# Ten expert units' down products as seven products instead of eight, summed in PSUM, in a one-core perceiver layer

## The chip, the cores and the metric

The kernel is one program on one NeuronCore of a Trainium2 chip. The metric is the device time of that program in microseconds (us). Three runs of the kernel before gave 785.26, 785.72 and 786.43 us, median 785.72 us. The profile shows one further execution, instruction by instruction.

Engines are named as the profile names them: PE is TensorE's matrix multiplication and PEld its loading of the stationary operand, DVE is VectorE, ACT is ScalarE, POOL is GpSimd, SP the engine that issues most DMAs. SBUF is the on-chip memory, PSUM the accumulators that PE writes (eight banks of 512 fp32 columns).

## The reference, cut to what matters

T = 256 tokens of width D = 512 go through three residual blocks: a sigmoid cross-attention over 25,088 context rows, a causal self-attention with 16 heads of 64, and a mixture of experts. Everything is fp32. The change lies in the third:

```python
gu = x @ shared_gate_up_w                                  # shared: 1024 hidden
shared = _silu(gu[:, :Is]) * gu[:, Is:] @ shared_down_w
shared = shared * jax.nn.sigmoid(x @ shared_gate_w)
probs = jax.nn.softmax((x @ gate_w).astype(jnp.float32), axis=-1)
w, idx = jax.lax.top_k(probs, TOP_K)                       # 8 of 64 experts a token
w = w / jnp.sum(w, axis=-1, keepdims=True)
...
gu_e = jnp.einsum('ech,ehf->ecf', buf, expert_gate_up_w)
act = _silu(gu_e[..., :I]) * gu_e[..., I:]                 # I = 256 hidden
out_e = jnp.einsum('eci,eih->ech', act, expert_down_w)
y = out_e[e_flat, slot] * w_flat[:, None]                  # weight of the token
return (y + shared).reshape(B, S, H)
```

## The kernel before, in words

The first 551 us of the trace are the cross-attention, the next 60 the self-attention; neither is edited. In the self-attention a loop over e = 0..7 (two heads each) is pipelined by two steps: `scored(e)` puts scores into PSUM, DVE takes maxima, ACT exponentials, `divided(e, t)` lets POOL divide the exponentials `pe` by their sums (two POOL instructions a step), and `turned(e)` transposes them on PE one step later. `queries(e + 2)` in the same loop is the last reader of the turned input `anT`.

The mixture of experts works in *units* of 256 hidden columns. The shared expert is cut into four, s0 to s3. The routed experts are ranked by how many tokens chose them; the eight fullest, e0 to e7, are run for all 256 tokens, and a token that did not choose an expert has weight 0 for it. The seven next are run on gathered tokens (`seated`, `gathered`, and the `few_...` functions, with rounds of 32-slot quarters).

A unit has two parts. `gate_up` makes the hidden columns of all tokens, already transposed, [128 hidden, 2 halves, 256 tokens]: 16 products with a 128x128 stationary operand and 256 moving columns into two PSUM banks `ph`, then a sigmoid on ACT and two multiplications on DVE into `hT`. `down` multiplies them with the unit's down matrix `dn`: for each of the two token tiles, two products of 512 columns into a bank `pd`, and one DVE instruction (L1189) that multiplies with the tokens' weights (a column of `wsh` or `wso`) and adds to `y`. `run` pipelines this by one unit: `gate_up(n + 1)` comes before `down(n)`. Its `between` entries put other work behind unit i: `counted` (count and rank the experts, then load e0 to e2), `permuted` (the weights transposed to `wT`, and put into the order of rank, `wso`), the few experts' steps.

The order on each engine is the scheduler's: instructions in `in_turn` (tc.keep_in_program_order) keep the program's order, the others are placed one by one by its estimates. On the chip every engine then works strictly in that order. A tile pool gives a tag a fixed number of buffers; who takes a buffer waits for the last readers of its former content. `work` holds two buffers a tag (`tok`, `tokT`), `wpool` three for `gu` and `dn`, so that dn of unit n + 3 is loaded (by SP, in SP's order) once `down(n)` is done. In PSUM, `bank` deals four single banks in turn (`among_three` and `apart`), `banks` two pairs.

Of the kernel before, what the change touches and what calls it, by code (L numbers as in the profile page):

```python
# [9 lines left out]
F32 = mybir.dt.float32  # L10
# [11 lines left out]
def tile_perceiver_layer(  # L22
# [730 lines left out]
    def banks(name):  # L753
        return pairs.tile([P, 2, 512], F32, tag="two", name=name)
# [7 lines left out]
    def bank(name):  # L762
        turns[1] += 1
        return apart(name) if turns[1] % 4 == 0 else among_three(name)
# [20 lines left out]
    QUARTERS = dict(sorted(part for places in ROUNDS for part in places))  # L785
    FEW = len(QUARTERS)
    GROUP = 16
    weights = {}
    late = ctx.enter_context(tc.tile_pool(name="late", bufs=1))
    wpool = ctx.enter_context(tc.tile_pool(name="wpool", bufs=3))  # L790
    hidden = ctx.enter_context(tc.tile_pool(name="hidden", bufs=3))

# [11 lines left out]
        return gu, dn  # L804

    SP, ACT = (nc.sync, mybir.EngineType.SP), (nc.scalar, mybir.EngineType.Activation)

    def load_expert(k, gu=None, dn=None, by=SP):

        queue, engine = by  # L810
        if gu is None:
            gu = wpool.tile([P, ND, 2 * I], F32, tag="gu", name=f"gu_{k}")
        if dn is None:
            dn = wpool.tile([P, NI, D], F32, tag="dn", name=f"dn_{k}")
        e = nc.values_load(
            order[0:1, k : k + 1],
            engines=[engine],
            min_val=0,
            max_val=E - 1,
            skip_runtime_bounds_check_because="the number has been cut to six bits",  # L820
        )
        queue.dma_start(
            gu, e_gate_up[bass.ds(e, 1)].rearrange("o (c p) f -> p (o c) f", p=P)
        )
        queue.dma_start(dn, e_down[bass.ds(e, 1)].rearrange("o (c p) f -> p (o c) f", p=P))
        return gu, dn

    for k in range(NS):
# [248 lines left out]
    few = ctx.enter_context(tc.tile_pool(name="few", bufs=1))  # L1077


    wt = late.tile([P, NT, E], F32, tag="wt", name="wt")  # L1080
    wsh = late.tile([P, NT, 1], F32, tag="wsh", name="wsh")
    chosen_all = late.tile([P, NT, E], F32, tag="chosen", name="chosen_all")
    pls = []

# [19 lines left out]
    def choose(t):  # L1104
        lg = pls[t]
        top = small.tile([P, TOPK], F32, tag="top", name=f"top_{t}")
        nc.vector.max(top, lg[:, 0:E])
        rest = small.tile([P, E], F32, tag="rest", name=f"rest_{t}")
        nc.vector.match_replace(rest, top, lg[:, 0:E], LOWEST)
        chosen = chosen_all[:, t, :]  # L1110
        nc.vector.tensor_tensor(chosen, rest, lg[:, 0:E], ALU.not_equal)
        ntop = small.tile([P, 1], F32, tag="ntop", name=f"ntop_{t}")
        nc.vector.tensor_scalar(ntop, top[:, 0:1], -1.0, None, ALU.mult)
        ex = small.tile([P, E], F32, tag="ex", name=f"ex_{t}")
        in_turn(nc.scalar.activation(ex, lg[:, 0:E], AF.Exp, bias=ntop))
        nc.vector.tensor_mul(ex, ex, chosen)
        es = small.tile([P, 1], F32, tag="es", name=f"es_{t}")
        nc.vector.tensor_reduce(es, ex, AX.X, ALU.add)
        rs = small.tile([P, 1], F32, tag="res", name=f"res_{t}")
        nc.vector.reciprocal(rs, es)  # L1120
        nc.vector.tensor_scalar(wt[:, t, :], ex, rs, None, ALU.mult)
    def gate_up_products(n, halves, lo, hi, mark=lambda ins: ins):
        gu, _ = weights[n]
        for half, ph in enumerate(halves):
            for f in range(NI):
                col = half * I + f * P
                for c in range(ND):
# [10 lines left out]
    def gate_up(n, tiles_done=None):  # L1138
# [10 lines left out]
        nc.scalar.activation(hf, pg, AF.Sigmoid)  # L1149
        nc.vector.tensor_mul(hf, pg, hf)  # L1150
        nc.vector.tensor_mul(hf, pu, hf)
        return hT

# [16 lines left out]
    LAST_PARTS = WIDE_PARTS[:-1] + [(NT - 1, lo, lo + D // 2) for lo in range(0, D, D // 2)]  # L1172

    def down(n, hT, parts=WIDE_PARTS):
        _, dn = weights.pop(n)
        nm = f"{n[0]}{n[1]}"
        for t, lo, hi in parts:
            pd = banks(f"pd_{nm}_{t}_{lo}")[:, 0, 0 : hi - lo]
            for f in range(NI):
                nc.tensor.matmul(  # L1180
                    pd,
# [28 lines left out]
    def counted():  # L1210
# [33 lines left out]
            nc.vector.tensor_max(left[:, 0:1], left[:, 0:1], left[:, 1:2])  # L1244
        nc.vector.tensor_mul(left[:, 0:1], left[:, 0:1], nact)
        nc.vector.tensor_copy(active, left[:, 0:1])
        for k in range(3):
            weights["e", k] = load_expert(k)

    def permuted():  # L1250
# [4 lines left out]
        nc.tensor.matmul(pp[0:E, :E], lhsT=onesrow_sb, rhs=of, start=True, stop=True)  # L1255
        perm = late.tile([E, E], F32, tag="perm", name="perm")
        nc.vector.tensor_scalar(perm, pp[0:E, :E], number_sb, None, ALU.is_equal)
        pt = bank("pt_wt")
        for t in range(NT):
            nc.tensor.transpose(pt[0:E, t * P : (t + 1) * P], wt[:, t, :], ident)  # L1260
        wT = late.tile([E, T], F32, tag="wT", name="wT")
        nc.vector.tensor_copy(wT, pt[0:E, :T])
        pw = bank("pw_wt")
        for t in range(NT):
            nc.tensor.matmul(
                pw[:, t * E : (t + 1) * E],
                lhsT=wT[:, t * P : (t + 1) * P],
                rhs=perm,
                start=True,
                stop=True,  # L1270
            )
        nc.vector.tensor_copy(wso.rearrange("p t e -> p (t e)"), pw[:, : NT * E])

    run([("s", k) for k in range(NS)], {0: counted, 2: permuted})

# [160 lines left out]

    def few_spread():
        for t in range(NT):  # L1440
            pd = banks(f"pd_few_{t}")[:, 0, :]
            for r in range(NR):
                nc.tensor.matmul(
                    pd,
# [129 lines left out]
```

## Time and profile before

| what | value |
|---|---|
| median of three runs | 785.72 us (785.26 to 786.43) |
| profiled execution, own time | 786.12 us |
| its span, first to last instruction | 784.3 us |
| granted TensorE clock, mean | 0.999 |
| PE busy | 771.3 us (98%) |
| PEld busy | 612.4 us (78%) |
| DVE busy | 548.4 us (70%) |
| ACT busy | 202.4 us (26%) |
| POOL busy | 154.4 us (20%) |
| mixture of experts | from about 618 us of the span to its end |

The profiled execution took 0.40 us more than the median, and 1.82 us more than its span. A matmul of the kernel is fp32 and shows as two MATMUL and two LDWEIGHTS records, so the 16 products of a `gate_up` are a row of x32, and the four of a `down` a row of x8. A matmul's own duration overlaps the next one's; the distance from start to start is read from the chain or the timeline. "[0.30 <-DVE rsm L970]" behind a row is the idle time of that engine before it, and what ended it.

### The profile page before, as it was taken

The page shows a single profiled execution, that of the slowest core. Times are in us where ns is not written, and L with a number is a line of the kernel's source. Part 1 is how long each engine was busy: PE and PEld are TensorE (multiplying, and loading weights), DVE is VectorE, ACT ScalarE, POOL GpSimd, SP SyncE. Part 2 cuts the span into 40 slices and gives each one's busy share as a digit, 9 for nine tenths or more (in the row PEclk, how much of TensorE's full clock was granted, in tenths as well). Part 3 has the DMA queues.
Part 4 walks back from the last instruction along what each step waited for, and adds up shares of the span by engine and source line. Part 5 has one row for each costly group of instructions (what it writes and reads, how often), then busy time and mean ns, then how long its engine had stood idle before and what let it go on. Part 6 is the DMA issues. An engine that isn't in the chain of part 4 may idle for free.

```text
span 784.3 us, 12147 instructions
## 1 busy us (share of the span) xinstructions
PE 771.3 (98%) x4008; PEld 612.4 (78%) x4008; DVE 548.4 (70%) x1597; ACT 202.4 (26%) x485; POOL 154.4 (20%) x304
## 2 busy tenths in 40 slices
PE   8999999999999999999999999999999999999996
PEld 6888888888888888888888888889675676775563
DVE  5978878888788887887888878876655553513222
ACT  4222222222222222222222222222445310110110
POOL 3222223223222232232222322222123000000000
PEclk9999999999999999999999999999999999999999
DMA  9999999998786877878778788740600033399400
GB/s 246 268 233 257 260 226 293 240 213 195 206 196 169 211 186 191 206 171 212 188 177 211 178 198 201 171 115 1 221 22 2 1 134 132 113 369 392 148 1 30
DMA packets 153797, 140.86 MB, mean 180 GB/s; under 512 B 9088, under 2 KB 113280, under 8 KB 153728
## 3 DMA queue, kind: packets, MB, share of 16 engines
q1 hardware_dynamic: 152992, 139.49, 69.6%
q8 instruction: 34, 0.56, 0.3%
q10 hardware_dynamic: 672, 0.52, 0.2%
q14 instruction: 35, 0.29, 0.1%
q0 software_dynamic: 64, 0.00, 0.0%
HBM read 139.47 MB, written 0.52 MB: 178 GB/s over the span
## 4 chain that ended last, share of the span: by engine, by line
PE 96%; DVE 2%; ACT 1%; POOL 1%; issue 0%; ACTq 0%
PE xacc L572 36%; PE pk L355 22%; PE pz L373 11%; PE ph_e L1129 7%; PE pd_e L1180 4%; PE ph_s L1129 3%; PE pd_s L1180 2%; PE pa L844 2%; PE ph_few L1398 1%; PE pw L908 1%; PE py L727 1%; PE ps L934 1%; PE pi L211 1%; PE ptp L985 1%; PE po_few L1429 1%; PE pf L1375 1%
## 5 line engine op out<-in xcount | busy, mean ns | idle before, releaser
L572 PE MATMUL xacc<-T,S 128*128 128x172 f32 (+2 forms) x912 | 185.5, 308 | 0.0
L355 PE MATMUL pk<-cT,wkT_sb 128*128 128x384 f32 x512 | 175.5, 486 | 0.0
L572 PEld LDWEIGHTS xacc<-T,S 128*128 128x128 f32 x912 | 152.6, 190 | 20.3
L355 PEld LDWEIGHTS pk<-cT,wkT_sb 128*128 128x128 f32 x512 | 97.1, 190 | 54.4
L539 DVE TENSOR_TENSOR T<-ctx 128x172 f32<-128x172 f32 (+1 forms) x262 | 113.5, 434 | 0.0
L319 DVE STREAM_TRANSPOSE cT<-quarters 128x1536 f32<-128x1536 f32 x64 | 113.3, 1771 | 0.0
L539 POOL TENSOR_TENSOR T<-ctx 128x172 f32<-128x172 f32 x65 | 32.1, 493 | 385.5 <-PE xacc L572 379.3
L539 DVE TENSOR_TENSOR S<-zT 128x128 f32<-128x128 f32 x196 | 56.3, 287 | 72.7 <-ACT zT L382 72.7
L373 PE MATMUL pz<-qT,kT 128*128 128x256 f32 x392 | 106.0, 379 | 0.7 <-ACT kT L364 0.7
L382 ACT ACTIVATE zT<-pz 128x256 f32<-128x256 f32 (+1 forms) x131 | 64.2, 490 | 114.1 <-PE pz L373 114.1
L572 PE MATMUL xacc<-T,zT 128*128 128x173 f32 (+1 forms) x396 | 89.9, 308 | 0.0
L572 PE MATMUL xacc<-ctx,S 128*128 128x172 f32 x392 | 78.5, 309 | 0.0
L539 DVE TENSOR_TENSOR S<-zT,S 128x128 f32<-128x128 f32 x325 | 76.2, 285 | 0.0
L364 ACT ACTIVATE kT<-pk,bk 128x384 f32<-128x384 f32 (+1 forms) x66 | 38.2, 578 | 146.9 <-PE pk L355 146.9
L549 ACT COPY T<-ctx 128x170 f32<-128x170 f32 (+1 forms) x130 | 43.2, 334 | 125.4 <-PE xacc L572 125.4
L539 POOL TENSOR_TENSOR T<-ctx,T 128x170 f32<-128x170 f32 (+1 forms) x130 | 72.4, 576 | 2.2 <-PE xacc L572 2.2
L373 PEld LDWEIGHTS pz<-qT,kT 128*128 128x128 f32 x392 | 68.6, 190 | 4.8 <-ACT kT L364 1.3
L539 DVE TENSOR_TENSOR T<-ctx,T 128x172 f32<-128x172 f32 x195 | 65.4, 360 | 8.2 <-PE xacc L572 1.5
L572 PEld LDWEIGHTS xacc<-T,zT 128*128 128x128 f32 x396 | 66.4, 190 | 0.1
L572 PEld LDWEIGHTS xacc<-ctx,S 128*128 128x128 f32 x392 | 62.8, 190 | 0.0
L572 PE MATMUL xacc<-ctx,zT 128*128 128x170 f32 (+1 forms) x264 | 59.5, 307 | 0.0
L1129 PE MATMUL ph_e<-fT,gu 128*128 128x256 f32 x256 | 57.9, 381 | 0.0
(237 smaller groups left out, 716.2 us busy)
## 6 DMA issues: line engine op xcount, KB each, us to landing
ctx<-in_context SPq DMA_DIRECT2D x65, 768.0 KB, 5.3
quarters<-in_context SPq DMA_DIRECT2D x256, 192.0 KB, 6.3
gu<-in_e_gate_up SPq DMA_DIRECT2D x12, 1024.0 KB, 7.9
dn<-in_e_down SPq DMA_DIRECT2D x11, 512.0 KB, 6.1
gu_s<-in_s_gate_up SPq DMA_DIRECT2D x8, 512.0 KB, 5.9
a_wqT<-in_a_wqT SPq DMA_DIRECT2D x1, 2048.0 KB, 15.3
a_wout<-in_a_woutT SPq DMA_DIRECT2D x1, 2048.0 KB, 10.4
dn_s<-in_s_down SPq DMA_DIRECT2D x4, 512.0 KB, 7.7
```

The costliest lines, as they stand in the source:

```text
L211: nc.tensor.matmul(pi, lhsT=idle_sb[:, 0:P], rhs=idle_sb, start=True, stop=True)
L319: in_turn(nc.vector.transpose(new_turned(g), q.rearrange("p b (c r) -> p c b r", r=R)))
L355: nc.tensor.matmul(pk, lhsT=w[:, c, :], rhs=cT[:, c, 0 : n // R, :].rearrange("p b r -> p (b r)"), start=(c == 0), stop=(c == ND - 1),)
L364: in_turn(nc.scalar.activation(kT[:, 0:n], pk, AF.Identity, bias=bk_sb))
L373: nc.tensor.matmul(pz[:, i * T : (i + 1) * T], lhsT=kT[:, at : at + P], rhs=qT, start=True, stop=True,)
L382: nc.scalar.activation(zT[:, blocks[0] : blocks[-1] + 1, :].rearrange("p j t -> p (j t)"), pz[:, 0 : len(blocks) * T], AF.Sigmoid, scale=1 ...
L539: in_turn(f(o_, a_, b_))
L549: in_turn(nc.scalar.copy(named[to][:, 0:n], named[x_][:, 0:n]))
L572: nc.tensor.matmul(banks_of_products[i][:, cols], lhsT=named[lhs], rhs=named[rhs][:, 0:n],  start=i not in opened, stop=(g == G - 1 and last),
L844: nc.tensor.matmul(pa[:, 0 : hi - lo], lhsT=a_wqT_sb[:, c, e * P : (e + 1) * P], rhs=anT[:, c, lo:hi], start=(c == 0), stop=(c == ND - 1),)
L1129: nc.tensor.matmul(ph[:, f * T + lo : f * T + hi], lhsT=gu[:, c, col : col + P], rhs=fT[:, c, lo:hi], start=(c == 0), stop=(c == ND - 1),)
L1180: nc.tensor.matmul(pd, lhsT=hT[:, f, t * P : (t + 1) * P], rhs=dn[:, f, lo:hi], start=(f == 0), stop=(f == NI - 1),)
```

## The change

For ten units, s1 to s3 and e0 to e6 (`SEVEN`), the down product of [256 tokens x 256 hidden] by [256 hidden x 512] is cut in two each way and done by the Strassen-Winograd scheme: seven products of 128x128 blocks by 128x256 blocks in place of eight. Four sums of blocks of `hT` (`S_OF_SEVEN`, on DVE, 128x128 each) and four sums of blocks of `dn` (`T_OF_SEVEN`, on POOL, 128x256 each) feed them.

The seven results are not combined unit by unit. They are summed over all ten units in PSUM, in `seven`, which takes both pairs of banks from s1 to e6, and combined once by `add_seven` (one ACT copy and eleven DVE sums into `y`) after e6. So the tokens' weights must be in the left operand: `hT` of a unit is multiplied with them, along the tokens, by one more DVE instruction. For it the weights, with the shared gate as a 65th column (`wsh` is now that column of `wt`), are transposed (`turn_weights`, in the middle of s1's `gate_up`; the transposes leave `permuted`), written to a DRAM tile from POOL's queue, and read back as one row spread over all partitions: from POOL's queue for s1 to s3, from SP's queue behind each expert's `dn` for e0 to e6. The rows lie in four rooms in the old `wqT_sb` and `wkT_sb`. The expert loads of e0 to e2 move from `counted` to behind unit s1 (`load_first`). s0, e7 and the few experts keep their products, now in `bank` instead of `banks`. The sums' buffers reuse `x`, `x1`, `tokT` and `tok`.

```diff
--- before.py
+++ after.py
@@ -785,8 +785,15 @@
     QUARTERS = dict(sorted(part for places in ROUNDS for part in places))
     FEW = len(QUARTERS)
     GROUP = 16
+    SEVEN = [("s", k) for k in range(1, NS)] + [("e", k) for k in range(WHOLE - 1)]
     weights = {}
+    scales = {}
     late = ctx.enter_context(tc.tile_pool(name="late", bufs=1))
+    dram = ctx.enter_context(tc.tile_pool(name="dram", bufs=1, space=bass.MemoryType.DRAM))
     wpool = ctx.enter_context(tc.tile_pool(name="wpool", bufs=3))
     hidden = ctx.enter_context(tc.tile_pool(name="hidden", bufs=3))
 
@@ -804,6 +811,18 @@
         return gu, dn
 
     SP, ACT = (nc.sync, mybir.EngineType.SP), (nc.scalar, mybir.EngineType.Activation)
+    weights_of_tokens = dram.tile([E + 1, T], F32, tag="weights_of_tokens", name="weights_of_tokens")
+    scale_rooms = [
+        w.rearrange("p c e -> p (c e)")[:, lo : lo + T]
+        for w in (wqT_sb, wkT_sb)
+        for lo in range(0, ND * QK, T)
+    ]
+    def spread(tile_, row):
+        return tile_.unsqueeze(1), weights_of_tokens[row, :].partition_broadcast(P)
 
     def load_expert(k, gu=None, dn=None, by=SP):
 
@@ -823,6 +842,9 @@
             gu, e_gate_up[bass.ds(e, 1)].rearrange("o (c p) f -> p (o c) f", p=P)
         )
         queue.dma_start(dn, e_down[bass.ds(e, 1)].rearrange("o (c p) f -> p (o c) f", p=P))
+        if ("e", k) in SEVEN:
+            sc = scales["e", k] = scale_rooms[1 + k % 3]
+            queue.dma_start(*spread(sc, bass.ds(e, 1)))
         return gu, dn
 
     for k in range(NS):
@@ -1077,8 +1099,9 @@
     few = ctx.enter_context(tc.tile_pool(name="few", bufs=1))
 
 
-    wt = late.tile([P, NT, E], F32, tag="wt", name="wt")
-    wsh = late.tile([P, NT, 1], F32, tag="wsh", name="wsh")
+    wt = late.tile([P, NT, E + 1], F32, tag="wt", name="wt")
+    wsh = wt[:, :, E : E + 1]
     chosen_all = late.tile([P, NT, E], F32, tag="chosen", name="chosen_all")
     pls = []
 
@@ -1118,10 +1141,26 @@
         nc.vector.tensor_reduce(es, ex, AX.X, ALU.add)
         rs = small.tile([P, 1], F32, tag="res", name=f"res_{t}")
         nc.vector.reciprocal(rs, es)
-        nc.vector.tensor_scalar(wt[:, t, :], ex, rs, None, ALU.mult)
+        nc.vector.tensor_scalar(wt[:, t, 0:E], ex, rs, None, ALU.mult)
+    wT = late.tile([E + 1, T], F32, tag="wT", name="wT")
+    def turn_weights():
+        pt = bank("pt_wt")
+        for t in range(NT):
+            nc.tensor.transpose(pt[0 : E + 1, t * P : (t + 1) * P], wt[:, t, :], ident)
+        nc.vector.tensor_copy(wT, pt[0 : E + 1, :T])
+        nc.gpsimd.dma_start(weights_of_tokens, wT)
+        nc.gpsimd.dma_start(*spread(scale_rooms[0], slice(E, E + 1)))
+        for k in range(1, NS):
+            scales["s", k] = scale_rooms[0]
     def gate_up_products(n, halves, lo, hi, mark=lambda ins: ins):
         gu, _ = weights[n]
         for half, ph in enumerate(halves):
+            if half > 0 and n == SEVEN[0]:
+                turn_weights()
             for f in range(NI):
                 col = half * I + f * P
                 for c in range(ND):
@@ -1149,7 +1188,111 @@
         nc.scalar.activation(hf, pg, AF.Sigmoid)
         nc.vector.tensor_mul(hf, pg, hf)
         nc.vector.tensor_mul(hf, pu, hf)
+        if n in SEVEN:
+            nc.vector.tensor_mul(hT, hT, scales.pop(n).unsqueeze(1).to_broadcast([P, NI, T]))
+            sums_of[n] = sums_for_seven(n, hT)
         return hT
+    S_OF_SEVEN = """
+        s0 a10 + a11
+        s1 s0 - a00
+        s2 a00 - a10
+        s3 a01 - s1
+    """
+    T_OF_SEVEN = """
+        t0 b01 - b00
+        t1 b11 - t0
+        t2 b11 - b01
+        t3 t1 - b10
+    """
+    PRODUCTS_OF_SEVEN = (
+        "p0 a00 b00",
+        "p1 a01 b10",
+        "p3 a11 t3",
+        "p4 s0 t0",
+        "p5 s1 t1",
+        "p6 s2 t2",
+        "p2 s3 b11",
+    )
+    SUMS_OF_SEVEN = """
+        y00 y00 + p0
+        u1 p0 + p5
+        y00 y00 + p1
+        u3 u1 + p4
+        y01 y01 + u3
+        y01 y01 + p2
+        u2 u1 + p6
+        u0 u2 - p3
+        y10 y10 + u0
+        u3 u2 + p4
+        y11 y11 + u3
+    """
+    HALF = D // 2
+    sums_of = {}
+    seven = []
+    def block(n, hT, dn, s, t, nm):
+        i, k = nm[1:2], nm[2:3]
+        if nm[0] == "a":
+            return hT[:, int(k), int(i) * P : (int(i) + 1) * P]
+        if nm[0] == "b":
+            return dn[:, int(i), int(k) * HALF : (int(k) + 1) * HALF]
+        return (s if nm[0] == "s" else t)[:, int(i), :]
+    def sums_for_seven(n, hT):
+        _, dn = weights[n]
+        where = "x" if SEVEN.index(n) % 2 else "x1"
+        s_ = act.tile([P, 4, P], F32, tag=where, name=f"s_{n[0]}{n[1]}")
+        t_ = work.tile([P, 4, HALF], F32, tag="tokT", name=f"t_{n[0]}{n[1]}")
+        for engine, text in ((nc.gpsimd, T_OF_SEVEN), (nc.vector, S_OF_SEVEN)):
+            for line in text.strip().splitlines():
+                to, x_, op, y_ = line.split()
+                f = engine.tensor_add if op == "+" else engine.tensor_sub
+                f(*(block(n, hT, dn, s_, t_, nm) for nm in (to, x_, y_)))
+        return s_, t_
+    def product_of_seven(nm):
+        i = int(nm[1])
+        return seven[i // 4][:, i % 4 // 2, i % 2 * HALF : (i % 2 + 1) * HALF]
+    def down_by_seven(n, hT):
+        _, dn = weights.pop(n)
+        s_, t_ = sums_of.pop(n)
+        if not seven:
+            seven.extend(banks(f"seven_{i}") for i in range(2))
+        for text in PRODUCTS_OF_SEVEN:
+            nm, lhs, rhs = text.split()
+            nc.tensor.matmul(
+                product_of_seven(nm),
+                lhsT=block(n, hT, dn, s_, t_, lhs),
+                rhs=block(n, hT, dn, s_, t_, rhs),
+                start=(n == SEVEN[0] and nm in ("p0", "p3", "p4", "p6")),
+                stop=(n == SEVEN[-1] and nm in ("p1", "p2", "p5", "p6")),
+            )
+        if n == SEVEN[-1]:
+            add_seven()
+    def add_seven():
+        u = work.tile([P, 4, HALF], F32, tag="tok", name="u_seven")
+        p5 = u[:, 0, :]
+        nc.scalar.copy(p5, product_of_seven("p5"))
+        def named(nm):
+            if nm[0] == "y":
+                return y[:, int(nm[1]), int(nm[2]) * HALF : (int(nm[2]) + 1) * HALF]
+            if nm[0] == "u":
+                return u[:, int(nm[1]), :]
+            return p5 if nm == "p5" else product_of_seven(nm)
+        for line in SUMS_OF_SEVEN.strip().splitlines():
+            to, x_, op, y_ = line.split()
+            f = nc.vector.tensor_add if op == "+" else nc.vector.tensor_sub
+            f(named(to), named(x_), named(y_))
 
 
 
@@ -1172,10 +1315,13 @@
     LAST_PARTS = WIDE_PARTS[:-1] + [(NT - 1, lo, lo + D // 2) for lo in range(0, D, D // 2)]
 
     def down(n, hT, parts=WIDE_PARTS):
+        if n in SEVEN:
+            down_by_seven(n, hT)
+            return
         _, dn = weights.pop(n)
         nm = f"{n[0]}{n[1]}"
         for t, lo, hi in parts:
-            pd = banks(f"pd_{nm}_{t}_{lo}")[:, 0, 0 : hi - lo]
+            pd = bank(f"pd_{nm}_{t}_{lo}")[:, 0 : hi - lo]
             for f in range(NI):
                 nc.tensor.matmul(
                     pd,
@@ -1244,6 +1390,8 @@
             nc.vector.tensor_max(left[:, 0:1], left[:, 0:1], left[:, 1:2])
         nc.vector.tensor_mul(left[:, 0:1], left[:, 0:1], nact)
         nc.vector.tensor_copy(active, left[:, 0:1])
+    def load_first():
         for k in range(3):
             weights["e", k] = load_expert(k)
 
@@ -1255,23 +1403,18 @@
         nc.tensor.matmul(pp[0:E, :E], lhsT=onesrow_sb, rhs=of, start=True, stop=True)
         perm = late.tile([E, E], F32, tag="perm", name="perm")
         nc.vector.tensor_scalar(perm, pp[0:E, :E], number_sb, None, ALU.is_equal)
-        pt = bank("pt_wt")
-        for t in range(NT):
-            nc.tensor.transpose(pt[0:E, t * P : (t + 1) * P], wt[:, t, :], ident)
-        wT = late.tile([E, T], F32, tag="wT", name="wT")
-        nc.vector.tensor_copy(wT, pt[0:E, :T])
         pw = bank("pw_wt")
         for t in range(NT):
             nc.tensor.matmul(
                 pw[:, t * E : (t + 1) * E],
-                lhsT=wT[:, t * P : (t + 1) * P],
+                lhsT=wT[0:E, t * P : (t + 1) * P],
                 rhs=perm,
                 start=True,
                 stop=True,
             )
         nc.vector.tensor_copy(wso.rearrange("p t e -> p (t e)"), pw[:, : NT * E])
 
-    run([("s", k) for k in range(NS)], {0: counted, 2: permuted})
+    run([("s", k) for k in range(NS)], {0: counted, 1: load_first, 2: permuted})
 
 
 
@@ -1438,7 +1581,7 @@
 
     def few_spread():
         for t in range(NT):
-            pd = banks(f"pd_few_{t}")[:, 0, :]
+            pd = bank(f"pd_few_{t}")
             for r in range(NR):
                 nc.tensor.matmul(
                     pd,
```

## The prediction

> **What bounds the kernel now.** I read the page's busy shares first, then the chain of waits, then the timelines of PE, POOL and DVE from 555 us on, since everything the change touches lies there.
>
> ```profile
> PE 771.3 (98%) x4008; PEld 612.4 (78%) x4008; DVE 548.4 (70%) x1597; ACT 202.4 (26%) x485; POOL 154.4 (20%) x304
> ```
>
> PE bounds it, in the experts' part too: there the chain of waits is PE almost without a break, and its rows give the price of the two kinds of product.
>
> ```profile
> 687.16 6.91 PE ph_e L1129 x32
> 694.06 3.43 PE pd_e L1180 x8
> ```
>
> Both rows are gapless. A record with 256 moving columns costs 6.91/32 = 0.216 us, one with 512 costs 3.43/8 = 0.429 us. So PE time that is taken away here shortens the kernel, unless PE then waits for something. The next question is where PE waits already, and who is just in time. The PE and POOL timelines of the self-attention show such a place:
>
> ```profile
> 590.01 1.89 PE L844 MATMUL pa<-anT,a_wqT 128*128 128x256 f32 x8
> 591.83 0.93 PE L934 MATMUL ps<-kk,aq 64*128 64x128 f32 x8
> 593.49 0.88 PE L985 MATMUL ptp<-ident,pe 128*128 128x128 f32 x6
> ```
>
> ```profile
> 591.60 0.61 POOL L971 TENSOR_TENSOR pe<-pe,rsm 128x256 f32<-128x256 f32 x1 [2.24 <-DVE rsm L970]
> 592.51 1.04 POOL L971 TENSOR_TENSOR pe<-pe,rsm 128x512 f32<-128x512 f32 x1 [0.30 <-DVE rsm L970]
> ```
>
> Step e = 4: POOL's second division ends at 593.55, and PE's second transpose, due at 593.63, reads it. POOL is busy 20% of the span, but here it has 0.1 us to spare. Last, the rows that price the DMAs that the change adds (columns: form, queue, count, size, us from issue to landing):
>
> ```profile
> bk<-in_bk POOLq DMA_DIRECT2D x1, 0.5 KB, 5.8
> bq<-in_bq POOLq DMA_DIRECT2D x1, 0.5 KB, 6.0
> bv<-in_bv SPq DMA_DIRECT2D x1, 256.0 KB, 11.3
> lno_g<-in_lno_g SPq DMA_DIRECT2D x1, 256.0 KB, 5.2
> out<-y SPq DMA_DIRECT2D x1, 256.0 KB, 2.1
> ```
>
> bk and bq are the only ones on POOL's queue; bv and lno_g are one row spread over all partitions, as the change reads the weights; out is a write to DRAM while nothing else moves.
>
> **The change, part by part.**
>
> *The products.* Per unit 4 products of 512 columns (8 records, 3.43 us) become 7 of 256 (14 records x 0.216 = 3.02 us). Their shape, 128x128 stationary and 256 moving, is that of `ph_e`, whose weight load of 190 ns is hidden under 0.216. Ten units: 10 x 0.41 = **-4.1 us**, all on the path. It is 12%, not more, because a unit's gate_up (6.9 us) is left alone.
>
> *The sums of dn on POOL.* Four instructions of 128x256 a unit; the POOL row of 128x256 has 0.61 us. For s3 and e0 to e6 they wait for `down` of two units before (buffer) and run then, 2.5 us, while PE has over 6.9 us of gate_up before it needs them: nothing. But in the built order those of s1 and s2 stand in the self-attention. Those of s1 come ahead of POOL's first division; dn of s1 is issued at 557.7 and lands 7.7 us later by the median, so they run from 565.4 to 568 in POOL's idle time up to 574.2: nothing. Those of s2 take the buffer of `anT`, so the first waits for the last `queries`, which PE ends at 591.9, and three of the four stand *between* the two divisions of e = 4. Behind the waiting instruction is the second division, and PE waits for that. Three x 0.61 and about 0.1 for the dependent one, from 592.25, end at 594.2; the division ends at 595.25, its PE reader starts 595.25 - 593.63 = **+1.6 us** late. Does it come back? e = 5 gains the 0.3 us that PE waited for POOL there, but `scored(6)` stands behind the late transposes, so its maxima, exponentials and divisions are 1.6 us late too, and PE waits for them at e = 6 again. Followed through DVE's and ACT's rows to the last step, the delay stays 1.5 to 1.6. With sums at 0.55 us (a 128x170 row has 0.576 beside a busy DVE) it is 1.4, at 0.75 us 2.0.
>
> *DVE.* Per unit two additions to y (0.75 each) go; one 128x512 multiplication (0.69) and four 128x128 sums (0.29) come: +0.35 us, under 6.9 us of gate_up. Where DVE is not ahead of PE this costs: behind e0, PE's transposes of `share` follow DVE's 28 small instructions. The multiplication and the four sums now stand in front of the first share, 0.60 + 4 x 0.21 from start to start (DVE's records overlap by about 0.09): every share is 1.45 us later. The built PE order puts six products of e1 before the first transpose, so PE waits some 0.5 us in that stretch beyond its work where it waited 0.2 to 0.5 before: **+0.3 us**; 0 if PE's other work covers it, 1.0 if each sum takes its full 0.29 and a wait for the one before.
>
> *The weights' way through DRAM.* It is new, and one unit needs it early. Transposes at half of s1's gate_up (633.3; `wt` is done at 629.5), `wT` copied by DVE by 634.5, a POOL write of 66 KB, then, waiting for its landing, a POOL read of 128 KB. The multiplication of s1 waits for that on DVE, and behind it stand s1's sums, the second addition of s0, everything of s2 and then `perm`: 0.69 + 3 x 0.29 + 0.75 + 0.29 + 3 x 0.69 + 4 x 0.29 + 0.27 = 6.1 us. PE needs `perm` at 650.9, behind two products of s3. So the read must land by 644.8: the two DMAs have **10.3 us**. Write: 2.1 us (out) to 5.8 (bk). Read: 3.4 (x_sb, 256 KB) to 11.3 (bv, behind a 1 MB load). At 634 to 645 three loads of 0.5 to 1 MB pass, so neither a quiet nor a full queue: I take 2.1 + 0.4 for POOL's longer issue (0.72 us) and 5.2 (lno_g), 7.7 us: **0**. The ends are 5.5 us (0) and 17.1 us (+6.8).
>
> The Trainium skill (DMA: Bandwidth & Descriptors, "Anatomy of one DMA — SWDGE (gpsimd) path") gives such a DMA about 2.0 us plus its bytes at 436 GB/s; by that estimate the chain takes 4.5 us and costs nothing, while bk's row says nearly three times as much for next to no bytes.
>
> *SP's queue.* The seven further spreads stand behind their dn, some 0.5 to 0.9 us of SP each. e0's first loads keep their places, since they wait for buffers of s1 as before. What queues behind (gu_e1 issued 651.3, needed 672; the few experts' first 685.9, needed 710) has over 10 us: nothing. Each spread waits only for a multiplication that its dn's wait for `down` implies.
>
> *PSUM.* `pd` of s0, the few and e7 move to the four single banks. Dealing them out again, each bank's last reader comes over 1 us before the next writer, as long as DVE keeps the times above: nothing.
>
> *The end.* `add_seven`: a 0.4 us ACT copy and eleven DVE sums of 0.42 (`hf`, 128x256 from PSUM), ready about 7.5 us after e7's gate_up. PE then still has 3.0 of e6, 5.15 of `few_spread` and 3.4 of e7's down, and the first bank that could block is written at 10.7: nothing. If it took over 3 us longer it would show.
>
> Sum: -4.1 + 1.6 + 0.3 = **-2.2 us**. Against the profiled execution (786.12, span 784.3) that is 783.9; it stood 0.4 above the median of 785.72, so for medians **783.5**, 0.28% faster. What a measurement can tell from no change is about 0.2%, 1.6 us: 784.1 and 787.3.
>
> **The rivals.**
>
> 1. *The s2 sums do not hold PE up* (division and transposes find slack that the rows hide). For it: PE works 98%, and other stretches gave way. Against: in-order POOL and 0.1 us of slack. -3.8: 781.9. Chance 0.12.
>
> 2. *The chain of DMAs at bk's and bq's price*, 11.8 us: +1.5, 785.0, no change. For it: the only rows on that queue. Against: they ran at the start, among full queues. 0.15.
>
> 3. *Slower: the same chain, with the read like bv's.* Place: s1's multiplication, with DVE's whole queue behind it and PE at `perm`. It decides from 10.3 + 2.2 = 12.5 us, and is slower by 0.2% from 14.1; at 17.1 us the time is 790.3, at 15 us 788.2. For it: a read of one row by 128 partitions is what bv was. Against: bv was queued behind 1 MB; lno_g and lno_b needed 5.2 and 6.6. 0.15. The Trainium skill (SBUF — State Buffer, "SBUF: two separate sides") would push this way: it says POOL's DMA descriptors cannot be written while DVE runs certain copies. No run here shows it yet.
>
> 4. *DVE bounds more than computed* (sums at 0.75 us on POOL, share at 1.0): -1.1, 784.6, no change. 0.10.
>
> **Chances and range.** Forecast 0.48, of which a tenth lies within 0.2% (its own range, by the bounds of the two stalls, is 783.0 to 784.6). Faster: 0.43 + 0.12 = 0.55; within: 0.15 + 0.10 + 0.05 = 0.30; slower: 0.15. The range leaves out rival 3 and a bit of rival 1: 781.9 to 786.4.
>
> **What would show it.** Right: `seven` records 0.216 us apart, x14 in 3.02 us; POOL with three sums between the e = 4 divisions, and PE idle about 1.6 us before `ptp` there, with `ph_first` that much later than 625.97; s1's spread landing within 10 us of the `wT` copy, and no idle PE before `pw_wt`; PE without a gap from e2 to the end. Wrong: PE idle before s1's first `seven` or before `pw_wt` (rivals 2, 3); the e = 4 transposes on time (rival 1); PE waiting for a DVE sum or for y at the end, which I priced at nothing.

## The result and the profile after

The changed kernel took 782.92 us (median of six runs, 782.88 to 783.18) against 786.14 us for the kernel before (six runs, 785.26 to 786.58): ratio 0.9961, 95% interval 0.9948 to 0.9974, so 0.4% faster. The profiled execution took 782.96 us, its span 781.2 us, at a mean granted clock of 0.998. The forecast was 783.5 us.

PE stays the bound; DVE and POOL have more to do (first part of the page of the changed kernel, busy us, share of the span, count):

```profile
PE 766.9 (98%) x4068; PEld 623.7 (80%) x4068; DVE 554.8 (71%) x1638; ACT 202.8 (26%) x486; POOL 183.7 (24%) x346
```

The chain of waits around e1 and e2 (start, us, what) has a unit's products at 3.02 us in 14 records where they were 3.43 in 8, and the same 6.91 of `gate_up`, without a break:

```profile
687.20 6.91 PE ph_e L1168 x32
694.11 3.02 PE seven L1269 x14
697.13 2.58 PE pf L1518 x8
699.71 6.91 PE ph_e L1168 x32
706.62 3.02 PE seven L1269 x14
```

Over six units, from the start of e1's `gate_up` to `pd_few`, PE took 82.07 us before (686.99 to 769.06) and 79.59 after (687.04 to 766.63): 0.413 us less a unit, 4.1 for ten.

The loss is where it was expected. POOL's timeline in the self-attention at e = 4 (start, us, engine, line, operation, count, idle time before):

```profile
591.40 0.61 POOL L993 TENSOR_TENSOR pe<-pe,rsm 128x256 f32<-128x256 f32 x1 [2.24 <-DVE rsm L992]
591.98 1.41 POOL L1255 TENSOR_TENSOR t_s<-dn_s 128x256 f32<-128x256 f32 x2
593.35 0.71 POOL L1255 TENSOR_TENSOR t_s<-dn_s,t_s 128x256 f32<-128x256 f32 x1
594.03 1.03 POOL L993 TENSOR_TENSOR pe<-pe,rsm 128x512 f32<-128x512 f32 x1
595.03 0.72 POOL L1255 TENSOR_TENSOR t_s<-t_s,dn_s 128x256 f32<-128x256 f32 x1
```

and PE's, in the same place:

```profile
592.50 0.87 PE L1027 MATMUL po<-pT,va 128*64 128x256 f32 x8
593.30 0.33 PE L1007 MATMUL ptp<-ident,pe 128*128 128x128 f32 x1
595.12 0.77 PE L1007 MATMUL ptp<-ident,pe 128*128 128x128 f32 x5 [1.49 <-POOL pe L993]
```

Three sums of s2 stand between the divisions, the second division starts at 594.03 where it started at 592.51, and five of the six transposes wait. From here to the end of the attention PE is 1.63 us late: from the first `pkk` to a `pw` near its end it took 46.32 us before (561.62 to 607.94) and 47.95 after (561.44 to 609.39).

The weights' way through DRAM did not reach PE. DVE copied `wT` by 635.45, POOL issued the write and the read at 635.75 and 638.02, and the multiplication of s1 started at 643.88: 8.4 us. DVE's timeline from there (DVE waits 3.23 us for the read itself; its two later waits, for PE, are the slack that was left) and the DMA rows (size in KB, us to landing):

```profile
643.88 0.69 DVE L1192 TENSOR_TENSOR hT_s<-hT_s,wqT 128x512 f32<-128x512 f32 x1 [3.23 <-DMA wqT<-weights_of_tokens]
...
648.52 0.69 DVE L1190 TENSOR_TENSOR hT_s<-ph_s,hT_s 128x512 f32<-128x512 f32 x1 [1.76 <-PE ph_s L1168]
...
651.80 0.28 DVE L1405 TENSOR_SCALAR perm<-pp,number_sb 64x64 f32<-64x64 f32 x1 [0.80 <-PE pp L1403]
```

```profile
wqT<-weights_of_tokens POOLq DMA_DIRECT2D x1, 128.0 KB, 5.8
weights_of_tokens<-wT POOLq DMA_DIRECT2D x1, 65.0 KB, 2.0
```

To compare kernels without the start and the end of an execution, which scatter, this table takes the distance on PE from the first `pkk` record (the self-attention's beginning, ahead of all that is changed) to the first record of the last `pd_e`, both from PE's timeline. "Behind DVE" is the time from the last DVE instruction's end to the end of the span.

| kernel | median us | ratio to before (95%) | `pkk` | last `pd_e` | distance | behind DVE |
|---|---|---|---|---|---|---|
| before | 786.14 | | 561.62 | 774.21 | 212.59 | 5.72 |
| before, again | 785.85 | 0.9999 (0.9990 to 1.0008) | 561.48 | 774.06 | 212.58 | 5.57 |
| changed | 782.92 | 0.9961 (0.9948 to 0.9974) | 561.44 | 771.78 | 210.34 | 5.29 |
| changed, again | 783.10 | 0.9960 (0.9947 to 0.9974) | 561.41 | 771.78 | 210.37 | 5.10 |
| own buffer | 781.76 | 0.9946 (0.9932 to 0.9960) | 561.41 | 770.11 | 208.70 | 5.67 |
| own buffer, again | 781.41 | 0.9948 (0.9934 to 0.9961) | 561.33 | 770.05 | 208.72 | 5.33 |
| eight products | 785.38 | 0.9994 (0.9984 to 1.0003) | 561.58 | 774.46 | 212.88 | 5.02 |
| single banks (from before) | 785.42 | 0.9992 (0.9982 to 1.0001) | 561.38 | 773.96 | 212.58 | 4.81 |
| longer chain | 783.58 | 0.9970 (0.9961 to 0.9980) | 561.18 | 772.54 | 211.36 | 4.83 |
| shares first | 781.90 | 0.9946 (0.9930 to 0.9961) | 561.51 | 771.04 | 209.53 | 4.83 |
| sums on DVE | 782.88 | 0.9956 (0.9941 to 0.9971) | 561.07 | 771.43 | 210.36 | 5.65 |

Twice the same kernel gives the same distance to 0.03 us, so a tenth of a microsecond can be read from it, where the times need half of one and more.

### The profile page after: what moved, and what is told of

It is laid out like the page before. It is cut to its first block, busy times and chain, and to the rows that moved or that the text cites. A ratio compares the mean times of both kernels' runs of the same rounds, so it can differ in the third digit from the quotient of the medians.

```text
span 781.2 us, 12389 instructions
## 1 busy us (share of the span) xinstructions
PE 766.9 (98%) x4068; PEld 623.7 (80%) x4068; DVE 554.8 (71%) x1638; ACT 202.8 (26%) x486; POOL 183.7 (24%) x346
## 4 chain that ended last, share of the span: by engine, by line
PE 95%; DVE 2%; ACT 1%; POOL 1%; issue 0%; ACTq 0%; DVEq 0%; POOLq 0%
PE xacc L572 36%; PE pk L355 22%; PE pz L373 11%; PE ph_e L1168 7%; PE seven L1269 4%; PE ph_s L1168 3%; PE ph_few L1541 1%; PE pa L866 1%; PE pw L930 1%; PE py L727 1%; PE pi L211 1%; PE po_few L1572 1%; PE pf L1518 1%; PE pd_few L1586 1%; PE ps L956 1%; ACT pe L981 0%
```

## The experiments

**The sums of s2 behind the attention.** The theory was that three POOL sums make the whole loss; one buffer's tag moves them.

```diff
-        t_ = work.tile([P, 4, HALF], F32, tag="tokT", name=f"t_{n[0]}{n[1]}")
+        t_tag = "tok" if n == ("s", 2) else "tokT"
+        t_ = work.tile([P, 4, HALF], F32, tag=t_tag, name=f"t_{n[0]}{n[1]}")
```

> The T sums of s2 get a buffer of the tag `tok` in place of `tokT`, so they do not wait for the last reader of `anT`, and in the built order they stand on POOL behind all divisions of the self-attention. Nothing else is moved. My theory (the 1.64 us that PE waits before the second transpose of e = 4 come from three of these sums on POOL, and are never given back): the second division of e = 4 follows the first at once, PE's five transposes start without the 1.49 us wait, the time is 782.9 - 1.6 = 781.3 us, within 780.9 to 781.7. Rival (the delay is given back later, or another engine is as late there): 782.6 to 783.2 us, the same as the changed kernel. Second rival (the sums, run later, come in the way of s1's or s2's experts instead): up to 784 us, with PE idle before `ph_s2` or `seven` of s2.

Measured 781.76 us, 0.06 above the expected range. On POOL (timeline of this kernel) the second division again follows the first, and all four sums stand behind the last division:

```profile
591.37 0.61 POOL L993 TENSOR_TENSOR pe<-pe,rsm 128x256 f32<-128x256 f32 x1 [2.24 <-DVE rsm L992]
592.28 1.04 POOL L993 TENSOR_TENSOR pe<-pe,rsm 128x512 f32<-128x512 f32 x1 [0.30 <-DVE rsm L992]
...
605.47 1.04 POOL L993 TENSOR_TENSOR pe<-pe,rsm 128x512 f32<-128x512 f32 x1 [0.30 <-DVE rsm L992]
606.46 1.41 POOL L1256 TENSOR_TENSOR t_s<-dn_s 128x256 f32<-128x256 f32 x2
```

and PE makes its six transposes in one go:

```profile
592.47 0.87 PE L1027 MATMUL po<-pT,va 128*64 128x256 f32 x8
593.27 0.87 PE L1007 MATMUL ptp<-ident,pe 128*128 128x128 f32 x6
```

The distance falls by 1.64 us, as much as the delay measured 1.63, and nothing of it comes back later. Since the two medians lay only 1.16 us apart and were taken beside different runs of the kernel before, both kernels were run once more, on one chip:

> The changed kernel itself, beside the next run on one chip, so that the two can be told apart. 782.9 us as before, ratio 0.996 to the kernel before.

> The kernel whose T sums of s2 have a buffer of their own, once more, beside the changed kernel on the same chip. My theory (three sums cost 1.6 us, which the trace of its first run shows from 593 us to the last matmul): 1.2 to 1.7 us below the changed kernel, 781.3 to 781.8 us, with an interval against the kernel before that lies wholly below that of the changed kernel. Rival (the trace's 1.67 us are made up for behind the last matmul): no difference.

783.10 and 781.41 us, 1.69 apart; the distances repeat (210.37 and 208.72). The two intervals against the kernel before still overlap a little (0.9947 to 0.9974, 0.9934 to 0.9961), so in that the expectation is not met; the distances tell the two apart. This kernel, at 0.9946 to 0.9948 of the kernel before, is better than both.

**Eight products, all else kept.** This takes away the seven products and their sums, and leaves the weights in the left operand, their way through DRAM, and the sum over ten units in PSUM.

```diff
-            sums_of[n] = sums_for_seven(n, hT)
...
-        for text in PRODUCTS_OF_SEVEN:
...
+        for t in range(NT):
+            for f in range(NI):
+                nc.tensor.matmul(
+                    seven[0][:, t, :],
+                    lhsT=hT[:, f, t * P : (t + 1) * P],
+                    rhs=dn[:, f, :],
+                    start=(n == SEVEN[0] and f == 0),
+                    stop=(n == SEVEN[-1] and f == NI - 1),
+                )
         if n == SEVEN[-1]:
-            add_seven()
+            for t in range(NT):
+                nc.vector.tensor_add(y[:, t, :], seven[0][:, t, :], y[:, t, :])
```

> The changed kernel with eight products of 128 columns stationary in place of seven: four matmuls of 512 columns a unit, added up over the ten units in one pair of PSUM banks, the weights still multiplied into the left operand by the same way through DRAM; no S and T sums on DVE and POOL, two additions to y at the end. It computes the same result. My theory (the gain is 0.41 us of PE a unit, and the loss is POOL's sums in the self-attention): ten times 0.41 come back (+4.1), the attention's wait goes (-1.6), of e0's stretch 0.1 to 0.3 goes: +2.2 to +2.5 on 782.9, so 785.1 to 785.4 us; PE's rows `seven` show 8 records in 3.43 us a unit. Rival (what gains is that y is no longer added to after each unit, and that the weights ride in the left operand): 783.0 us or less, with PE gapless where the kernel before has waits.

Measured 785.38 us, 2.46 above the changed kernel; the distance is 2.54 longer. That is 4.12 for the products less 1.64 for the attention, and 0.06. The chain of waits has the old price, on the new accumulator:

```profile
687.40 6.91 PE ph_e L1168 x32
694.31 3.43 PE seven L1267 x8
```

Against the kernel before the distance is 0.29 longer: the new way of the weights and the sum in PSUM gain nothing between the attention and the last unit, and 0.22 of the 0.29 lie in e0's stretch (`pn` to the first `pf`: 672.13 to 684.41, 12.28 us, before; 672.16 to 684.66, 12.50 us, here).

**Single banks for the last unit, in the kernel before.** The changed kernel's last PE row is 0.24 us shorter, which the prediction had not counted. In the kernel before, the third tile of e7's products waited for one of the two pairs of banks (its PE and PEld timelines):

```profile
774.21 3.85 PE L1180 MATMUL pd_e<-dn,hT_e 128*128 128x512 f32 x12
776.93 0.73 PEld L1180 LDWEIGHTS pd_e<-dn,hT_e 128*128 128x128 f32 x4 [0.38 <-DVE y L1189]
```

```diff
-            pd = banks(f"pd_{nm}_{t}_{lo}")[:, 0, 0 : hi - lo]
+            if parts is LAST_PARTS:
+                pd = bank(f"pd_{nm}_{t}_{lo}")[:, 0 : hi - lo]
+            else:
+                pd = banks(f"pd_{nm}_{t}_{lo}")[:, 0, 0 : hi - lo]
```

> The kernel before, with the last unit's down products in the four single banks in place of the two pairs, as the changed kernel has them. My theory (of PE's last 3.85 us, 0.25 to 0.38 was a wait of the third tile for one of two pairs, which the changed kernel no longer has): PE's last `pd_e` records follow each other without the 0.38 us idle before the third, and the span is 0.25 us shorter; in time 785.9 against 786.1, which the rounds alone can hardly tell, so the profile's row decides. Rival (the wait for y only moves to the last addition, so that the end of the last output is the same): records gapless, the last DVE instruction no earlier.

PE's last row falls from 3.85 to 3.61 us, and the last DVE instruction waits 0.38 us for PE where it waited 0.63 (timelines of this kernel, PE and DVE):

```profile
773.96 3.61 PE L1183 MATMUL pd_e<-dn,hT_e 128*128 128x512 f32 x12
```

```profile
777.61 0.48 DVE L1192 SCALAR_TENSOR_TENSOR y<-pd_e,wso,y 128x256 f32<-128x256 f32 x1 [0.38 <-PE pd_e L1183]
```

From the first `pkk` to the start of the last DVE instruction it is 216.23 us against 216.48. So this part of the change is worth 0.25 us, and the rival falls. The median was 0.55 us below that of the kernel before on the same chip (785.97), but the interval reaches 1.0001, and what the time shows beyond the 0.25 lies behind DVE (below).

**A longer way for the weights.** Two copies from DRAM to DRAM are put into it, to find at what length PE begins to wait.

```diff
-        nc.gpsimd.dma_start(weights_of_tokens, wT)
+        nc.gpsimd.dma_start(hops[0], wT)
+        nc.gpsimd.dma_start(hops[1], hops[0])
+        nc.gpsimd.dma_start(weights_of_tokens, hops[1])
```

> The changed kernel with two further copies from DRAM to DRAM on POOL's queue between the write of the tokens' weights and the read that spreads them. The way through DRAM took 8.1 us; by the changed kernel's DVE rows it may last 2.7 us longer, 10.8, before `perm` is late. Each further copy takes 2 to 4 us by the write's row (2.0 us to land, 0.3 from landing to the next issue), so the way lasts 12.7 to 16.7 us. My theory (in-order DVE behind s1's multiplication holds back `perm`, or PE's first `seven`, from 10.8 us on, one for one): 782.9 + 1.9 to 5.9 = 784.8 to 788.8 us, with PE idle before `seven` of s1 or before `pw_wt` for as long as the way exceeds 10.8. Rival (nothing of PE hangs on that way, or the wait is given back): 782.9 us.

Measured 783.58 us, below the expected range, since the way was shorter than expected. It took 11.96 us, from the copy's end at 635.21 to the multiplication at 647.17; that is 3.5 us longer and not 4.6 to 8.6, because the last read landed in 3.3 us where it had needed 5.8. PE waits at the place foretold (its timeline, then DVE's and POOL's ahead of it):

```profile
653.51 0.66 PE L1413 MATMUL pw_wt<-perm,wT 64*128 64x64 f32 x4 [0.93 <-DVE perm L1410]
```

```profile
650.02 0.69 DVE L1197 TENSOR_TENSOR hT_s<-hT_s,wqT 128x512 f32<-128x512 f32 x1
650.75 1.04 DVE L1260 TENSOR_TENSOR s_s<-hT_s 128x128 f32<-128x128 f32 x2
651.72 0.81 DVE L1260 TENSOR_TENSOR s_s<-s_s,hT_s 128x128 f32<-128x128 f32 x1
652.57 0.69 DVE L1260 TENSOR_TENSOR s_s<-hT_s,s_s 128x128 f32<-128x128 f32 x1
653.19 0.27 DVE L1410 TENSOR_SCALAR perm<-pp,number_sb 64x64 f32<-64x64 f32 x1
```

```profile
650.93 1.45 POOL L1260 TENSOR_TENSOR t_s<-dn_s 128x256 f32<-128x256 f32 x2 [6.55 <-PE seven L1274]
```

The distance grew by 1.02 us and the median by 0.66. So PE does hang on that way, and the rival falls. But the wait is not bare lateness, passed on one for one as expected (which would put its beginning at 11.96 - 0.93 = 11.0 us). The four S sums of s2 now met POOL's T sums of s3 (from 650.93 on) and took 2.5 us, from 650.75 to 653.26, against 1.0 in the changed kernel; less these 1.5 us, `perm` would have started at 651.7 and been done before PE came to it at 652.58. At what length between 8.4 and 12.0 us PE begins to wait is therefore not shown. Whether POOL slowed the sums is the subject of the next experiment.

**The sums of dn on DVE.** In the changed kernel the S sums of e1 had also been slow (684.82 to 687.78), and those of e2 not (695.60 to 696.61), with POOL at its T sums from 684.27 to 687.64 in the first case and only from 696.78 in the second. DVE's timeline of the changed kernel:

```profile
684.82 1.43 DVE L1255 TENSOR_TENSOR s_e<-hT_e 128x128 f32<-128x128 f32 x2
686.17 0.81 DVE L1255 TENSOR_TENSOR s_e<-s_e,hT_e 128x128 f32<-128x128 f32 x1
687.01 0.77 DVE L1255 TENSOR_TENSOR s_e<-hT_e,s_e 128x128 f32<-128x128 f32 x1
...
695.60 0.49 DVE L1255 TENSOR_TENSOR s_e<-hT_e 128x128 f32<-128x128 f32 x2
```

and POOL's in the slow stretch:

```profile
684.27 1.82 POOL L1255 TENSOR_TENSOR t_e<-dn 128x256 f32<-128x256 f32 x2 [14.82 <-PE seven L1269]
```

```diff
-        for engine, text in ((nc.gpsimd, T_OF_SEVEN), (nc.vector, S_OF_SEVEN)):
+        of_t = nc.vector if n[0] == "e" else nc.gpsimd
+        for engine, text in ((of_t, T_OF_SEVEN), (nc.vector, S_OF_SEVEN)):
```

> The changed kernel with the T sums of e0 to e6 on DVE in place of POOL; those of s1 to s3 stay on POOL, so the wait in the self-attention stays too. The question is why DVE's four S sums of e1 took 3.0 us in the changed kernel where those of e2 took 1.05. My theory (DVE and POOL, both adding from two SBUF operands, hinder each other): with POOL idle e1's S sums take 0.28 us each again, and so does every other unit's; DVE has 1.7 us more a unit, far below the 6.9 us of gate_up, so the time stays within 0.4 us of the changed kernel's 782.9. Rival (something else slows e1's sums, the DMAs that land then, for one): they keep 0.7 to 0.8 us each.

782.88 us, and a distance of 210.36: the same. With nothing on POOL, e1's S sums are as fast as all others (DVE's timeline of this kernel), and a T sum takes 0.42 us where POOL needs 0.72:

```profile
684.34 0.42 DVE L1256 TENSOR_TENSOR t_e<-dn 128x256 f32<-128x256 f32 x1
684.68 0.49 DVE L1256 TENSOR_TENSOR s_e<-hT_e 128x128 f32<-128x128 f32 x2
685.08 0.28 DVE L1256 TENSOR_TENSOR s_e<-s_e,hT_e 128x128 f32<-128x128 f32 x1
```

So the two engines hinder each other, and the rival falls. It costs nothing in the changed kernel, since PE needs e1's sums only at 693.94. For e0 to e6, DVE could have made the T sums at no cost.

**The shares of e0 first.** From the own-buffer kernel, with e0's multiplication and S sums behind DVE's last `share`.

```diff
-        if n in SEVEN:
-            nc.vector.tensor_mul(hT, hT, scales.pop(n).unsqueeze(1).to_broadcast([P, NI, T]))
-            sums_of[n] = sums_for_seven(n, hT)
+        if n == ("e", 0):
+            later.append((n, hT))
+        elif n in SEVEN:
+            weigh(n, hT)
         return hT
+    later = []
+    def weigh(n, hT):
+        mark = in_turn if n == ("e", 0) else lambda ins: ins
+        mark(nc.vector.tensor_mul(hT, hT, scales.pop(n).unsqueeze(1).to_broadcast([P, NI, T])))
+        sums_of[n] = sums_for_seven(n, hT)
...
-                    nc.vector.tensor_scalar(
-                        share[:, t, r, first : first + n],
+                    in_turn(
+                        nc.vector.tensor_scalar(
+                            share[:, t, r, first : first + n],
...
+        for n, hT in later:
+            weigh(n, hT)
         for r in range(NR):
             pt = bank(f"pt_share_{r}")
```

> The kernel whose T sums of s2 have a buffer of their own, and besides, for e0 alone, the multiplication by the weights and the four sums stand behind the last `share` instruction on DVE, so that the first share is ready 1.3 us earlier, as in the kernel before; PE's seven products of e0 move behind e1's gate_up. The step under test is the +0.3 us that the prediction charged for shares that are late. By the prediction: 0.3 us come back, the stretch from `pn` to the first `pf` falls from 12.02 to 11.7 us, 781.3 us or less. Rival (PE has other products to do meanwhile, so lateness of the shares costs next to nothing; only the wait for `rank` remains): the stretch stays within 0.15 us of 12.02, or grows by the 0.4 us for which the fourth and fifth transposes stand back to back in this order; 781.4 to 782.0 us.

In the changed kernel PE's timeline of this stretch has one wait only, for `rank` (0.29 us; the kernel before waits 0.21 for `hT_e` there), and products of e1 and of e0 (`seven`) between the transposes:

```profile
673.46 2.86 PE L1168 MATMUL ph_e<-fT,gu 128*128 128x256 f32 x12 [0.29 <-DVE rank L1474]
676.15 0.27 PE L1510 MATMUL pt_share<-ident,share 128*128 128x128 f32 x1
...
677.24 0.59 PE L1269 MATMUL seven<-dn,hT_e 128*128 128x256 f32 x2
677.68 0.33 PE L1510 MATMUL pt_share<-ident,share 128*128 128x128 f32 x1
```

Here the first transpose of a share comes 2.42 us after `pn` (670.88 to 673.30) instead of 3.71 (672.44 to 676.15), and yet the stretch grew from 12.02 to 12.84 us and the distance by 0.82. There is one wait more for a share and one for ACT's copy of a transposed share, because e0's seven products now stand behind everything and no longer between the transposes (PE's timeline of this kernel):

```profile
671.91 1.56 PE L1168 MATMUL ph_e<-fT,gu 128*128 128x256 f32 x6 [0.30 <-DVE rank L1483]
...
676.42 0.33 PE L1523 MATMUL pt_share<-ident,share 128*128 128x128 f32 x1 [0.24 <-DVE share L1504]
677.02 1.13 PE L1168 MATMUL ph_e<-fT,gu 128*128 128x256 f32 x4 [0.27 <-ACT shareT L1524]
```

Around these two waits, from 675.91 to 677.02, two transposes take 0.51 and 0.60 us from start to start, where the others take 0.11 to 0.17; that makes up the 0.8 us. So the prediction's reading falls. The rival had the direction, but half the size (0.4). The edit moved both the shares and e0's products; what cost time here is the work that no longer stands between the transposes. The medians (781.90 against 781.41 and 781.76) point the same way, but cannot show it.

**The kernel before, once more.** The medians differ by 3.2 us, and the distance and PE's last row account for 2.25 + 0.24 = 2.5.

> The kernel before itself, as one more of its runs, for its profile. Between the first `pkk` and PE's last matmul the changed kernel is 2.5 us shorter, its median 3.2 us; 0.6 us lie before `pkk` (561.62 against 561.44 us) and behind the last DVE instruction (5.72 against 5.29 us). My theory (these two are scatter from run to run, none of the change): this profile has `pkk` anywhere from 561.0 to 561.7 and 4.8 to 5.8 us behind the last DVE instruction, with the same 212.6 us between `pkk` and the first of the last `pd_e`; the ratio is 1.000. Rival (the kernel before has a longer end, of the output's DMA for one): again 5.6 us or more.

`pkk` came at 561.48, inside the scatter. Behind the last DVE instruction lie 5.57 us, inside the theory's range and 0.03 short of the rival's, so this profile does not tell the two apart. The slowest of the three output DMAs needed 3.5 and 3.3 us to land in the two profiles of the kernel before, 3.3 and 3.2 in those of the changed kernel, and between 2.0 and 3.7 in the others; in the three where it landed in 2.6 us or less (single banks, the longer chain, the shares first), 4.81 to 4.83 us lie behind DVE, in the rest 5.02 to 5.72. The end is shortest where that DMA is fastest.

The medians speak against the theory. The kernel before had 786.14 us beside the changed kernel, 785.97 beside the own buffer, eight products, single banks and the longer chain, and 786.34 beside the four others. In all nine rows the median lies further below these than the distance and the 0.25 us of the last row explain, by 0.1 to 1.1 us and 0.7 on average. Scatter from run to run would fall on both sides, and the kernel before differs from itself by 0.1 us only (785.85 against 785.93). So the kernel before seems longer outside the compared stretch as well; no trace shows where. On average over the profiles it has 0.2 us more ahead of `pkk` and 0.5 behind DVE, both no larger than the spread of single profiles.

## Why the prediction was right

783.5 us were forecast, 782.9 measured. That they lie so close is in part luck: the forecast starts from a median of 785.72, and from the 786.14 of six runs the same -2.2 gives 783.9. The gain was 3.2 us, not 2.2. Between `pkk` and the last unit the terms are -4.12, +1.64 and +0.15, which give -2.33 where the distance shows -2.25; the end adds -0.25.

- *The products, -4.1.* Right: 14 records in 3.02 us, ten times, -4.12. The experiment with eight products puts all of it on the products.
- *POOL's sums in the attention, +1.6.* Right in place, mechanism and size (1.63 in the trace, 1.64 by undoing it). Two details were off against each other: a sum takes 0.70 to 0.72 us, not 0.61, but the first started at 591.98 and not at 592.25, so that the close agreement in size is in part luck. That the delay would stay to the end, which the prediction followed through DVE's and ACT's rows, held. The sign named for it, `ph_first` that much later than 625.97, came out smaller, 1.0 us: two records of s1's gate_up, 0.43 us, no longer stand ahead of it on PE, and this profile's `pkk` is 0.18 earlier.
- *e0, +0.3.* Mis-sized, and for the wrong reason. The stretch became 0.26 us shorter, 12.28 to 12.02; with 0.41 less of products that is +0.15. The shares were 1.24 us later against `pn` (1.45 had been computed), but PE waits for none of them: its only wait in the stretch is for `rank`, and the scheduler's order puts products of e1 and e0 between the transposes. In the kernel with eight products the shares are only 0.53 us later, and the stretch is 0.22 longer, so their lateness does not set the size. Making them early again cost 0.8 us.
- *The weights' way, 7.7 us and no cost.* Right: 8.4 us, no cost. The limit of 10.3 us came out too early: at 11.96 us, where it would give a wait of 1.7, PE waited 0.93, and by the rows above it would not have waited without the slow sums. The Trainium skill (DMA: Bandwidth & Descriptors, "Anatomy of one DMA — SWDGE (gpsimd) path") gives 2.0 us plus the bytes at 436 GB/s. By that estimate the write takes 2.15 us, and the trace agrees, with 2.0; for the read it gives 2.3, and the runs show 5.8 and 3.3. The 4.5 us by the Trainium skill for both together were too few, the rows of other DMAs nearer.
- *The end, nothing.* Missed in the other direction: the step on PSUM looked only for new waits, and not for the one that single banks take away, 0.25 us. `add_seven` itself stayed hidden, done at 770.7, as PE went through the few experts' products.
- *DVE, SP's queue, the T sums elsewhere, nothing.* Right for the time: PE shows no wait in s1 to s3 and none from e2 to e7. That a sum of DVE takes 0.7 to 0.8 us beside POOL's sums was not foreseen; in the changed kernel it costs nothing.

Of the rivals, 1 (the sums don't hold PE up) fell with the own buffer, 2 and 3 (a chain of 11.8 us and more) with the 8.4 us measured; that PE hangs on such a chain the longer one shows, at 12.0 us and together with the slow sums. Rival 4 was half true: sums near 0.75 us on POOL, but no greater loss.

Left open: about 0.7 of the 3.2 us between the medians, outside the stretch that the traces compare. The same remainder shows in the other kernels.

## What to carry to other kernels

A buffer's tag decides when work may start and so where a scheduler puts it; helper instructions that share an in-order engine with work on the critical path should take a buffer whose last reader is not in the middle of that work. Here one tag gave back 1.6 us of the 4.1 that the seven products save. When work is taken from a stretch that is full of short waits, look at what the remaining order leaves between those waits before moving a "late" instruction forward: making the shares early lost more than their lateness had cost, since other products moved with them. And distances between two marks in the trace repeat to 0.03 us where medians of one kernel lie up to half a microsecond apart.

## What the runs showed of the hardware

DVE and POOL slow each other when both add two operands from SBUF. A DVE sum of 128x128 took 0.28 us beside an idle POOL and 0.69 to 0.81 beside a POOL sum, close to that sum's own 0.72 to 0.77; the pair of POOL sums took 1.82 instead of 1.41. With the T sums moved to DVE, and POOL idle, the effect was gone. The Trainium skill (SBUF — State Buffer, "SBUF: two separate sides") states that a DVE instruction with two SBUF inputs and a POOL instruction that reads SBUF take one pair of ports in turn, each for its whole length; these numbers agree. The other effect that the Trainium skill names there, POOL's DMA descriptors held up by DVE's copies, no run here tests: beside POOL's write, which landed in 2.0 us, DVE's timeline has only a product that reads PSUM and instructions on one partition.

The same read by POOL's queue, one row of DRAM into 128 partitions, landed in 5.6 to 5.9 us in seven runs, and in 3.3 in the longer chain, which issued it 5.8 us later than the changed kernel; why is not shown. SP's spreads of the same size took a median of 3.5 to 6.9 over the runs.
